# A four-layer attention kernel: the weighted sums of the one-head layer as seven products in three of four batches, joins taken ahead on the vector engine

## The chip, the core and the metric

The kernel is one program on one core of a Trainium2 chip. The core has a matrix engine (PE, with its weight loads shown as PEld), a vector engine (DVE), an activation engine (ACT), a general engine (POOL) and a queue for transfers (SP). [...] The metric is the device time of one execution in microseconds (us), as the median of some runs. A separate profiled execution gives the times of the single instructions. All data are float32.

## What is computed

The input x is [4, 512, 32, 32]: four batches of 512 channels by 1024 places. Four layers follow one another: attention with 8 heads, a linear attention, attention with one head after a layer normalisation, and attention with 4 heads after a group normalisation. The change lies in the third layer:

```python
def _L2_conv_ref(x, norm_w, w_qkv, b_qkv, w_proj, b_proj):
    b, c, h, w = x.shape
    xf = jnp.transpose(x, (0, 2, 3, 1)).reshape(b, h * w, c)
    mu = jnp.mean(xf, axis=-1, keepdims=True)
    var = jnp.var(xf, axis=-1, keepdims=True)
    xn = (xf - mu) * jax.lax.rsqrt(var + EPS) * norm_w
    qkv = jnp.einsum('bnc,dc->bnd', xn, w_qkv) + b_qkv
    q, k, v = jnp.split(qkv, 3, axis=-1)
    scale = c ** (-0.5)
    attn = jax.nn.softmax(jnp.einsum('bqc,bkc->bqk', q, k) * scale, axis=-1)
    out = jnp.einsum('bqk,bkc->bqc', attn, v)
    out = jnp.einsum('bnc,dc->bnd', out, w_proj) + b_proj
    out = jnp.transpose(out.reshape(b, h, w, c), (0, 3, 1, 2))
    return x + out
```

For one batch the weighted sum `attn @ v` is a product of a 1024 x 1024 matrix and a 1024 x 512 matrix.

## The kernel before

`plain_path` runs the layers one after the other, and within a layer batch after batch. The third layer is the loop over batches at L1555; its attention is `one_head` (L1128). There the projections are folded together beforehand: `gq` is the product of the query and key weights, `hv` that of the value and output weights. So a batch of this layer has four stages on PE:

1. `seven_products` with `gq`: the transformed queries `q` (PE line L701).
2. `project_v` (which calls `seven_products`): the values `vt`, already through the output weights (L819).
3. `seven_products` in `one_head`: the scores, keys by queries (L826). As soon as a block of scores is whole, `exp` puts its exponential in its place (ACT, L1146) and adds it to a running sum `acc` (DVE, L1149), from which the row sums come.
4. the weighted sums (L1168): a loop over 2 halves of the queries (`qb`) and 4 blocks of 128 output channels (`m`); each of its eight rounds is a chain of 8 matrix products of 128 x 128 by 128 x 512, one for each tile of 128 keys. After the first round two more products with `ones` spread the row sums over the partitions (L1175). DVE then inverts them (`invert`: a reciprocal L673 and two maxima L675 and L676 for a check), multiplies each round's result by the inverse (L1181) and adds bias and residual into x (L1183).

`seven_products` is a scheme in which a product of matrices of 2 x 2 blocks takes seven block products and not eight: `sum_inputs` and `sum_weights` make sums and differences of blocks (t[0..3] and s[0..3]), `p1` to `p7` are the block products, and DVE joins their results (L730 in `join`, L766 in `p6`, L771 in `p7`). It is used in stages 1 to 3; stage 4 is a direct product.

PE is scheduled by hand: `tc.manual_schedule(engines={PE})` keeps the order in which the program calls matrix products. For the other engines a scheduler picks, out of what is ready by its own clock, by a priority that follows the program's order. Small pieces of other work are put between PE's products in two ways: a list `pieces`, of which `slot()` takes one, and in `one_head` a list `parts`, of which one is taken ahead of each of the eight rounds. In stage 4 the parts are the layer normalisation of the next batch (`layer_norm`: `add`, `center`, `scale`, for each half), then `sum_inputs` for it; in the last batch the first group normalisation of the next layer, the load of that layer's weights `wqkv3` and the sum `weighted_bias("bo3", ...)`.

On chip memory is full, so tiles are shared by tags: the scores lie in the four "pt" tiles, the two "sum" tiles and the "wo" tile; `places`, the sums of the query blocks, lie before the change in the tile `after` that the next batch's normalisation writes. PSUM has four accumulator tiles of 512 columns (`acc_tile`) and two of twice that size (`two_tile`). Between batches `away(b)` stores x of a batch to a home in memory and `back` loads another one in its place (SP queue).

The two lines of stage 4 that matter most:

```python
out, lhsT=v[j // 2][:, j % 2, bass.ts(m, P)], rhs=pts[j][:, qb, :],
start=(i == 0), stop=(i == NT - 1),
```

Of the kernel before, what the change touches and what calls it, by code (L numbers as in the profile page):

```python
# [18 lines left out]
P = 128  # L19
# [455 lines left out]
def plain_path(ctx: ExitStack, tc: tile.TileContext, d: dict, out: bass.AP, count):  # L475
# [23 lines left out]
    def acc_tile():  # L499
        return ps_acc.tile([P, TB], F32, tag="acc", name="acc")  # L500
# [21 lines left out]
    def chunks_tile(tag, name, bufs=1):  # L522
        return work.tile([P, NC, TB], F32, tag=tag, bufs=bufs, name=name)
# [134 lines left out]

    idle = lambda: None

    def both(*fs):
        return lambda: [f() for f in fs]

# [41 lines left out]
    def seven_products(  # L705
# [20 lines left out]

        def join(out, ps, i, o, other):

            if bias is None:
                nc.vector.tensor_tensor(out, view(ps), other, ALU.add)  # L730
            else:
                joined[:] = [stt(out, view(ps), bias(i, o), other, ALU.add, ALU.add).ins]

        def p1(o, ms=(0, 1)):
            if 0 in ms:
# [27 lines left out]
        def p6(o):  # L763
            ps = acc_tile()
            mult(o, ps, made[o][1], t[1])
            nc.vector.tensor_tensor(dst(0, 1, o), dst(0, 1, o), view(ps), ALU.add)  # L766

        def p7(o):
            seven[o] = acc_tile()
            mult(o, seven[o], made[o][2], t[2], stop=False)  # L770
            nc.vector.tensor_tensor(dst(1, 1, o), dst(0, 1, o), view(seven[o]), ALU.add)  # L771


        if first:
# [350 lines left out]
        while parts:  # L1125
            parts.pop(0)()

    def one_head(b, q, ws, acc, keys, sums, v, scale, bias, parts):  # L1128

        x = xs[b]
        wide = wpool.tile([P, NC, C], F32, tag="wo", name="pts")
        pts = [pt_tile("pt") for _ in range(4)] + [sum_tile("pt") for _ in range(2)]
        pts += [wide[:, 2 * i : 2 * i + 2, :] for i in range(2)]

        order = [j for o in range(NC) for j in (o, o + NC)]  # L1140
        pts = dict(zip(order, pts))
        taken = []

        def exp(tb, o):
            pt = pts[tb * NC + o]
            nc.scalar.activation(pt, pt, AF.Exp, scale=scale)  # L1146
            taken.append(pt)
            if len(taken) > 1:
                nc.vector.tensor_tensor(acc, acc if len(taken) > 2 else taken[0], pt, ALU.add)  # L1149

        seven_products(
            NC,
            lambda i, j, o: q[i][:, 2 * j : 2 * j + 2, :],
            keys,
            None,
            lambda i, tb, o: pts[tb * NC + o][:, i, :],
            lambda: sums,
            lambda o: ws,
            keys_first,
            done=exp,  # L1160
        )
        quotients = chunks_tile("q0", "rd")
        for n, (qb, m) in enumerate(itertools.product(range(NTB), range(NC))):
            if parts:
                parts.pop(0)()
            out = acc_tile()
            for i, j in enumerate(order):
                nc.tensor.matmul(  # L1168
                    out, lhsT=v[j // 2][:, j % 2, bass.ts(m, P)], rhs=pts[j][:, qb, :],
                    start=(i == 0), stop=(i == NT - 1),  # L1170
                )
            if n == 0:
                ps = two_tile("rowsum")
                for t in range(NTB):
                    nc.tensor.matmul(  # L1175
                        ps[:, t, :], lhsT=ones, rhs=acc[:, t, :], start=True, stop=True
                    )
            if m == 0:
                invert(quotients[:, qb, :], ps[:, qb, :])
            t = quotients[:, NTB + n % 2, :]  # L1180
            nc.vector.tensor_tensor(t, out, quotients[:, qb, :], ALU.mult)  # L1181
            xv = x[:, m, bass.ts(qb, TB)]
            nc.vector.scalar_tensor_tensor(xv, t, bias[:, m : m + 1], xv, ALU.add, ALU.add)  # L1183
        assert not parts

# [168 lines left out]
    def layer_norm(b, tb, tiles):  # L1356

        x = xs[b][:, :, bass.ts(tb, TB)]
        t = {}

        def add():
            s = t["s"] = row_tile("s")
            nc.vector.tensor_tensor(s, x[:, 0, :], x[:, 1, :], ALU.add)
            for c in range(2, NC):
                nc.vector.tensor_tensor(s, s, x[:, c, :], ALU.add)

        def center():
            xn = tiles[tb]
            t["ps"] = two_tile("lnsums")
            mean = t["ps"][:, 0, :]  # L1370
            nc.tensor.matmul(mean, lhsT=ones, rhs=t["s"], start=True, stop=True)
            for c in range(NC):
                nc.vector.scalar_tensor_tensor(
                    xn[:, c, :], mean, -1.0 / C, x[:, c, :], ALU.mult, ALU.add
                )
            for c in range(NC):
                sq = row_tile("sq")
                nc.scalar.activation(sq, xn[:, c, :], AF.Square)
                if c == 0:
                    t["sq"] = sq  # L1380
                else:
                    nc.vector.tensor_tensor(t["sq"], t["sq"], sq, ALU.add)

        def scale():
            xn = tiles[tb]
            var = t["ps"][:, 1, :]
            nc.tensor.matmul(var, lhsT=ones, rhs=t["sq"], start=True, stop=True)
            rstd = row_tile("rstd")
            nc.scalar.activation(rstd, var, AF.Sqrt, bias=eps, scale=1.0 / C)
            nc.vector.reciprocal(rstd, rstd)  # L1390
            for c in range(NC):
                nc.vector.scalar_tensor_tensor(
                    xn[:, c, :], xn[:, c, :], col("nw2", c), rstd, ALU.mult, ALU.mult
                )

        return [add, center, scale]


    affine = {}
# [61 lines left out]
    with tc.manual_schedule(engines={mybir.EngineType.PE}):  # L1461
# [66 lines left out]
        lin = linear_attention(B - 1, lambda i: pt_tile("l1"))  # L1528

        norms[1][0]()  # L1530
        pieces.extend([norms[0][2], norms[1][1], *lin[:2], norms[1][2], idle, *lin[2:]])
        gq = chunks_tile("ot", "gq")
        for o in range(NC):
            ps = gps.get(o)
# [20 lines left out]
        for b in range(B):  # L1555
            q = q_tiles()
            vt = v_tiles()
            after = normed_tiles(b + 1)

            def sums():  # L1560
                if b == 0:
                    made.extend(sum_inputs(spare, normed(xn)))
                return made

            half = NC // 2
            seven_products(
                half,
                lambda i, j, o: gq[:, 2 * j : 2 * j + 2, bass.ts(i * half + o, P)],
                normed(xn),
                lambda i, o: uq[:, i * half + o : i * half + o + 1],  # L1570
                lambda i, tb, o: q[tb][:, i * half + o, :],
                sums,
                slots=2,
            )


            pair = lambda t, i: t[:, 2 * i : 2 * i + 2, :]
            places = [pair(after[0], 0), pair(after[0], 1), pair(after[1], 0), pair(q[1], 0)]
            query_sums = lambda: sum_weights(places, lambda i, j: pair(q[i], j))
            if b > 0:  # L1580
                query_sums()
            project_v(vt, hv, normed(xn), made, wpool.tile([P, NC, C], F32, tag="wo", name="ws"))
            flush()
            if b == 0:

                query_sums()
                away(B - 1)
                back(2)
            if b + 1 < B:
                norms = [layer_norm(b + 1, tb, after) for tb in range(NTB)]  # L1590
                (add0, *n0), (add1, *n1) = norms
                add0()
                parts = [
                    n0[0], idle, both(n0[1], add1), idle, n1[0], idle, n1[1],
                    lambda: sum_inputs(spare, normed(after)),
                ]
            else:
                first = chunks_tile("ot", "gn")

                def load3():  # L1600
                    return load_wqkv(d["wqkv3"]), load_bias(
                        d["bv3"], d["wo3n"],
                        [after[1][:, 2 * i : 2 * i + 2, :] for i in range(2)],
                    )

                loads3 = []
                norm = group_norm(0, 0, first)
                parts = [
                    idle, both(lambda: loads3.extend(load3()), norm[0]), *norm[1:],
                    lambda: loads3.append(weighted_bias("bo3", loads3.pop())),  # L1610
                ]
            one_head(
                b, q, places, pair(after[1], 1), normed(xn), made, vt, float(C) ** -0.5, bo2, parts
            )
            away(b)
            back((b + 3) % B)
            if b + 1 < B:
                xn = after
# [103 lines left out]
```

## Time and profile before

| what | us |
|---|---|
| median of 3 runs | 2511.36 |
| lowest and highest of them | 2510.95, 2512.14 |
| the profiled execution, its own time | 2511.6 |
| span in its profile, first to last instruction | 2509.5 |
| DVE busy in the span | 1606.4 |
| ACT busy | 705.3 |
| POOL busy | 255.2 |

The profiled execution took 2511.6 us, 2.1 us more than the span from its first to its last instruction, and 0.24 us more than the median of the runs. A matrix product in float32 is two entries of the profile, each of them with its own weight load. "Busy" of PE counts the time in which at least one product is under way; the entries overlap at their ends, so that the start-to-start distance, and not the length of an entry, is the price of one more product. The granted clock of PE is full (1.000) over the whole span.

### The profile page before, as it was taken

The numbers are of one execution on the slowest core, as the hardware profiler recorded it, in microseconds if no ns is written. First come the engines' busy times: TensorE is split into PE (matmuls) and PEld (weight loads), VectorE is DVE, ScalarE is ACT, GpSimd is POOL, SyncE is SP. The second block draws the span as 40 slices with busy tenths as digits, with TensorE's granted clock in tenths as the row PEclk, the third lists the DMA queues.
The fourth block names the chain that finished last, engine by engine and source line by source line (L and its number), as shares of the span: only waits on it lengthen the run. The fifth ranks groups of instructions, "written<-read, shape, count | busy, mean of one in ns | idle before, by whom it ended". The sixth has DMA issues, their size and how long they took to land.

```text
span 2509.5 us, 24916 instructions
## 1 busy us (share of the span) xinstructions
PE 2489.5 (99%) x10266; PEld 1286.6 (51%) x10266; DVE 1606.4 (64%) x1815; ACT 705.3 (28%) x859; POOL 255.2 (10%) x240
## 2 busy tenths in 40 slices
PE   9999999999999999999999999999999999999998
PEld 4545544554455454644645446446556456555653
DVE  3788588758875888657275463644664773565465
ACT  1454155315531643221120211102321320321121
POOL 4001100110020001102103011021010001002000
PEclk9999999999999999999999999999999999999999
DMA  5000010001000301011001010110000000000000
GB/s 214 1 1 1 5 68 1 1 5 68 1 1 17 115 1 51 5 67 56 12 1 67 0 70 2 67 67 17 17 31 20 1 17 17 1 17 17 0 9 26
DMA packets 23304, 72.46 MB, mean 29 GB/s; under 512 B 1809, under 2 KB 9489, under 8 KB 21137
## 3 DMA queue, kind: packets, MB, share of 16 engines
q1 hardware_dynamic: 23184, 70.82, 7.7%
q8 instruction: 82, 1.34, 0.2%
q14 instruction: 38, 0.30, 0.0%
HBM read 44.60 MB, written 25.17 MB: 28 GB/s over the span
## 4 chain that ended last, share of the span: by engine, by line
PE 96%; DVE 3%; issue 1%; ACT 0%; DMA 0%; SPq 0%; DVEq 0%; ACTq 0%
PE acc L701 19%; PE acc L819 12%; PE acc L1168 9%; PE acc L951 9%; PE sc L913 9%; PE sc L908 8%; PE acc L936 8%; PE acc L826 7%; PE acc L1013 6%; PE acc L963 1%; PE acc L971 1%; PE feat L638 1%; DVE sum L924 1%; PE acc L638 1%; DVE rd L673 1%; PE acc L1260 1%
## 5 line engine op out<-in xcount | busy, mean ns | idle before, releaser
L917 ACT ACTIVATE pt<-sc 128x1024 f32<-128x1024 f32 x384 | 380.3, 1023 | 631.7 <-PE sc L913 372.7
L924 DVE TENSOR_TENSOR sum<-sum,pt 128x1024 f32<-128x1024 f32 x256 | 313.2, 1224 | 46.7 <-ACT pt L917 35.3
L936 PE MATMUL acc<-pt,v 64*64 64x512 f32 x2048 | 291.1, 590 | 0.0
L908 PE MATMUL sc<-q,k 64*64 64x512 f32 x2048 | 273.9, 591 | 1.1 <-ACT pt L917 1.1
L913 PE MATMUL sc<-q,k 128*128 128x512 f32 x512 | 240.0, 593 | 0.7 <-ACT pt L917 0.7
L951 PE MATMUL acc<-pt,v 128*128 128x512 f32 x512 | 239.9, 592 | 0.0
L689 POOL TENSOR_TENSOR ws<-wqkv 128x256 f32<-128x256 f32 (+1 forms) x40 | 40.8, 1021 | 1343.2 <-PE acc L963 552.3
L673 DVE RECIPROCAL rd<-acc 128x512 f32<-128x512 f32 x32 | 107.4, 3357 | 107.4 <-PE acc L971 107.4
L701 PE MATMUL acc<-t,ws 128*128 128x512 f32 x384 | 173.9, 593 | 0.0
L1168 PE MATMUL acc<-pt,v 128*128 128x512 f32 x384 | 170.2, 592 | 0.0
L936 PEld LDWEIGHTS acc<-pt,v 64*64 64x64 f32 x2048 | 104.2, 133 | 121.3 <-issue 98.3
L908 PEld LDWEIGHTS sc<-q,k 64*64 64x64 f32 x2048 | 101.1, 133 | 123.6 <-issue 92.4
L951 PEld LDWEIGHTS acc<-pt,v 128*128 128x128 f32 x512 | 97.3, 190 | 122.5 <-issue 120.5
L913 PEld LDWEIGHTS sc<-q,k 128*128 128x128 f32 x512 | 96.7, 190 | 113.8 <-issue 87.9
L1168 PEld LDWEIGHTS acc<-pt,v 128*128 128x128 f32 x384 | 72.8, 190 | 90.9 <-issue 89.2
L701 PEld LDWEIGHTS acc<-t,ws 128*128 128x128 f32 x384 | 72.5, 190 | 86.6 <-issue 84.9
L673 DVE RECIPROCAL rd<-rs 128x512 f32<-128x512 f32 x32 | 107.3, 3353 | 1.1
L921 DVE TENSOR_TENSOR sum<-pt 128x1024 f32<-128x1024 f32 x64 | 76.7, 1198 | 42.7 <-ACT pt L917 42.7
L739 ACT COPY v<-acc 128x512 f32<-128x512 f32 x24 | 14.1, 586 | 287.9 <-PE acc L819 287.9
L730 DVE TENSOR_TENSOR v<-acc,v 128x512 f32<-128x512 f32 x72 | 49.7, 691 | 65.9 <-PE acc L819 65.7
L819 PE MATMUL acc<-ws,t 128*128 128x256 f32 x384 | 87.3, 379 | 0.0
L826 PE MATMUL acc<-q,ln 128*128 128x512 f32 x192 | 85.9, 593 | 0.8 <-DVE pts L730 0.8
(272 smaller groups left out, 3513.0 us busy)
## 6 DMA issues: line engine op xcount, KB each, us to landing
home<-x SPq DMA_DIRECT2D x8, 2048.0 KB, 6.3
x<-home SPq DMA_DIRECT2D x8, 2048.0 KB, 7.9
out<-x SPq DMA_DIRECT2D x32, 256.0 KB, 2.1
x<-in_x SPq DMA_DIRECT2D x3, 2048.0 KB, 16.9
wo<-in_wo SPq DMA_DIRECT2D x3, 1024.0 KB, 5.4
w<-in_w SPq DMA_DIRECT2D x1, 3072.0 KB, 17.6
wqkv<-in_wqkv SPq DMA_DIRECT2D x1, 3072.0 KB, 11.3
wqkv<-in_wqkv SPq DMA_DIRECT2D x2, 1024.0 KB, 9.6
```

Of the source, the lines that this page charges most:

```text
L673: nc.vector.reciprocal(rd, ps)
L701: nc.tensor.matmul(ps, lhsT=w[:, m, :], rhs=x[:, m, :], start=start, stop=stop, skip_group_check=True)
L819: nc.tensor.matmul(ps[:, bass.ts(r, C // 2)], lhsT=x[:, m, bass.ts(2 * o + r, P)], rhs=w[:, m, :], start=(start and r == 0), stop=stop, sk ...
L826: nc.tensor.matmul(ps, lhsT=x[:, m, bass.ts(o, P)], rhs=w[:, m, :], start=start, stop=stop, skip_group_check=True,)
L908: nc.tensor.matmul(ps[half(h), s, :], lhsT=key(g, i)[half(s), half(h)], rhs=q[qb][half(s), g, :], start=True, stop=True,)
L913: nc.tensor.matmul(ps[:, s, :], lhsT=key(g, 2 * i + s), rhs=q[qb][:, g, :], start=True, stop=True)
L917: exps.append(nc.scalar.activation(pt, ps, AF.Exp, scale=scale).ins)
L924: nc.vector.tensor_tensor(acc, acc, pt, ALU.add)
L936: nc.tensor.matmul(outs[qb, g][r][half(s), :], lhsT=v[i // 2][half(r), i % 2, g * P + s * hd : g * P + (s + 1) * hd], rhs=pt[half(r), s, : ...
L951: nc.tensor.matmul(outs[qb, g][0], lhsT=v[j // 2][:, j % 2, bass.ts(g, P)], rhs=pt[:, s, :], start=(j == 0), stop=(j == NT - 1),)
L1013: nc.tensor.matmul(ps[i][:, bass.ts(o, n)], lhsT=w[:, m, bass.ts(o, P)], rhs=t[:, m, :], start=(start and m + o == 0), stop=(stop and m == ...
L1168: nc.tensor.matmul(out, lhsT=v[j // 2][:, j % 2, bass.ts(m, P)], rhs=pts[j][:, qb, :], start=(i == 0), stop=(i == NT - 1),)
```

## The change

- In batches 1, 2 and 3 of the third layer, stage 4 becomes a scheme of seven block products: the blocks are two halves of the keys, two halves of the queries and two halves of the output channels. Each block product is a chain of 4 matrix products of 128 x 128 by 128 x 512 for each of two blocks of 128 output channels. Batch 0 keeps the direct product with its `parts`.
- The sums and differences of the blocks are made on DVE (`each`): 16 instructions of 128 x 256 for the values, 16 of 128 x 512 for the exponentials. They are put into tiles that are free by then (`xn`, `room`, the query tiles) or in place.
- The row sums come after `p1` and `p2` (after 16 products, where it was after 8); the four blocks' results are joined in SBUF (`add`), multiplied and added to x by `add_block`.
- In batches 1 and 2 the next batch's layer normalisation moves from stage 4 to `pieces`, taken from stage 2 on; `sum_inputs` for the next batch comes after stage 4. In batch 3 the group normalisation, the load of the bias weights and `weighted_bias` move there too; the load of `wqkv3` stays at the start of stage 4.
- The query sums `places` and the running sum `acc` get tiles of their own. `layer_norm` splits `scale` into `spread` and `scale`.
- The joins in all of `seven_products` (L730, L766, L771 before) and the `add`s are issued under `soon()`, which raises their priority for the scheduler.

The core of the diff:

```diff
+    soon = lambda: tc.high_priority(offset=300)
...
-            if bias is None:
-                nc.vector.tensor_tensor(out, view(ps), other, ALU.add)
-            else:
-                joined[:] = [stt(out, view(ps), bias(i, o), other, ALU.add, ALU.add).ins]
+            with soon():
+                if bias is None:
+                    nc.vector.tensor_tensor(out, view(ps), other, ALU.add)
+                else:
+                    joined[:] = [stt(out, view(ps), bias(i, o), other, ALU.add, ALU.add).ins]
...
+        n = C // 2
+        quotients = [xn[1][:, t, :] for t in range(NTB)]
+        temps = [xn[0][:, t, :] for t in range(4)]
+        d, e = temps[:2], temps[2:]
+        quarter = lambda t: t.rearrange("p a (r m) -> p (a r) m", m=n)
+        ws = [quarter(t) for t in (xn[1][:, 2:4, :], room[1][:, :2, :], room[1][:, 2:4, :])]
+        ts = [chunks_tile("q0", "ts"), room[0], None, chunks_tile("q1", "ts")]
+        weights = lambda i, j: [v[2 * j + m // 2][:, m % 2, i * n : (i + 1) * n] for m in range(4)]
+        inputs = lambda j, tb: [pts[4 * j + m][:, tb, :] for m in range(4)]
...
+        def each(out, a, b, op):
+            for args in zip(out, a, b):
+                nc.vector.tensor_tensor(*args, op)
...
+            for m in range(4):
+                nc.tensor.matmul(
+                    ps[i, o], lhsT=w[m][:, bass.ts(o, P)], rhs=t[m],
+                    start=(start and m == 0), stop=(stop and m == 3), skip_group_check=True,
+                )
...
+        def p3(o):
+            mult(5, o, s4, inputs(1, 1), start=False)
+            add(d[o], d[o], ps[5, o])
+            finish(0, 1, o, d[o], d[o])
+        def p4(o):
+            mult(7, o, weights(1, 1), t4, start=False)
+            add(e[o], d[o], ps[7, o])
+            finish(1, 0, o, e[o], e[o])
+        def p5(o):
+            mult(5, o, s1, t1, stop=False)
+            add(e[o], e[o], ps[5, o])
+            finish(1, 1, o, e[o], e[o])
+        def p6(o):
+            mult(6, o, s2, t2)
+            add(d[o], d[o], ps[6, o])
+        def p7(o):
+            mult(7, o, s3, t3, stop=False)
+            add(e[o], d[o], ps[7, o])
+        p1(0)
+        p1(1)
+        each(s1, weights(1, 0), weights(1, 1), ALU.add)
+        each(s2, s1, weights(0, 0), ALU.subtract)
+        each(t1, inputs(0, 1), inputs(0, 0), ALU.subtract)
+        each(t2, inputs(1, 1), t1, ALU.subtract)
+        p2(0)
+        p2(1)
+        rows = row_sums()
+        for t in range(NTB):
+            invert(quotients[t], rows[:, t, :])
+        for o in range(2):
+            finish(0, 0, o, e[o], ps[1, o])
+        each(s3, weights(0, 0), weights(1, 0), ALU.subtract)
+        each(t3, inputs(1, 1), inputs(0, 1), ALU.subtract)
+        each(t4, inputs(1, 0), t2, ALU.subtract)
+        each(s4, weights(0, 1), s2, ALU.subtract)
+        for f, o in [
+            (p6, 0), (p7, 0), (p6, 1), (p5, 0), (p4, 0), (p7, 1), (p3, 0), (p5, 1), (p4, 1), (p3, 1)
+        ]:
+            f(o)
...
-        return [add, center, scale]
+        return [add, center, spread, scale]
...
+            halves = work.tile([P, 2, 2, TB], F32, tag="os", name="qs")
+            third = work.tile([P, 2, TB], F32, tag="oi", name="qs")
+            places = [halves[:, 0], halves[:, 1], third, pair(q[1], 0)]
+            sum_weights(places, lambda i, j: pair(q[i], j))
...
+            elif b + 1 < B:
+                pieces.extend([
+                    add0, n0[0], idle, n0[1], n0[2], add1, n1[0], idle, n1[1], n1[2],
+                ])
             else:
                 first = chunks_tile("ot", "gn")
...
+                pieces.extend([
+                    *group_norm(0, 0, first),
+                    lambda: loads3.append(weighted_bias("bo3", loaded3)),
+                ])
...
+            if 0 < b < B - 1:
+                sum_inputs(spare, normed(after))
             away(b)
             back((b + 3) % B)
```

## The prediction

> **What bounds the kernel now.** I read the busy shares first, then the chain that ended last, then PE's instructions in order of time in the stage that changes.
>
> ```profile
> PE 2489.5 (99%) x10266; PEld 1286.6 (51%) x10266; DVE 1606.4 (64%) x1815; ACT 705.3 (28%) x859; POOL 255.2 (10%) x240
> ...
> PEclk9999999999999999999999999999999999999999
> ...
> PE 96%; DVE 3%; issue 1%; ACT 0%; DMA 0%; SPq 0%; DVEq 0%; ACTq 0%
> ```
>
> PE is busy for all but 20 us of the span, at full clock, and the chain runs through PE for 96%. A share of 99% can hide gaps between pipelined entries, so I look at the starts, here from the end of the scores of batch 2 to the next batch's first products (start, length, what, how many entries):
>
> ```profile
> 1431.07 1.02 PE L1371 MATMUL lnsums<-s,ones 128*128 128x512 f32 x2
> 1431.92 5.31 PE L1168 MATMUL acc<-pt,v 128*128 128x512 f32 x12
> 1437.07 1.88 PE L1168 MATMUL acc<-pts,v 128*128 128x512 f32 x4
> 1438.79 1.88 PE L1175 MATMUL rowsum<-ln,ones 128*128 128x512 f32 x4
> ...
> 1491.15 7.03 PE L701 MATMUL acc<-ln,gq 128*128 128x512 f32 x16
> ```
>
> From 1431.92 to 1438.79 are 16 entries, so one entry costs 0.429 us and one product (two entries) 0.858 us. From 1431.07 to 1491.15, 60.08 us, there are 8 rounds of 16 entries, 4 of row sums and 8 of the normalisation: 140 x 0.429 = 60.06. There is no gap at all: the stage costs what its number of products costs. [...]
>
> DVE's load and its relation to PE, by stretch (scores, then weighted sums, of batch 2) and by price:
>
> ```profile
> 1382.90:1431.07 48.17, 48.17 (x115) 21.36 (x114) 19.07 (x25) 13.04 (x16) 0.00 (x0) 1.00 0.00 0
> 1431.07:1491.15 60.08, 60.08 (x142) 26.60 (x140) 48.20 (x54) 9.08 (x13) 2.33 (x2) 1.00 0.01 5
> ```
> ```profile
> L673 DVE RECIPROCAL rd<-rowsum 128x512 f32<-128x512 f32 x8 | 26.8, 3354 | 10.5 <-PE rowsum L1175 10.5
> ...
> L766 DVE TENSOR_TENSOR pt<-pt,acc 128x512 f32<-128x512 f32 x12 | 8.3, 688 | 63.2 <-PE acc L826 63.2
> ...
> L1309 DVE TENSOR_TENSOR kxt<-kxh 128x256 f32<-128x256 f32 x8 | 3.0, 420 | 2.2 <-ACT kxh L1305 2.2
> ```
>
> The third number is DVE: 19.07 of 48.17 us in the scores, 48.20 of 60.08 in the weighted sums. So DVE is loaded in just the stage that gets more of its work.
>
> **The change, part by part.**
>
> *Products removed.* The weighted sums of a batch are 8 x 8 = 64 products; seven block products are 7 x 2 x 4 = 56. Row sums and normalisation keep their number, the latter only moves. So 8 products in each of 3 batches go: 24 x 0.858 = 20.6 us. As this stage has no gap, they come off the span unless PE waits for something new.
>
> *The sums on DVE.* Each batch gets 16 instructions of 128 x 512 and 16 of 128 x 256, and 10 joins. Back to back the starts are closer than the lengths: three starts in a row in this stage are 1456.62, 1457.22 and 1457.83, 0.60 us apart at 0.69 us each; a pair of the 128 x 256 form takes 0.75 us, so 0.33 for one more. The question is whether all sums are done when the row sums are, because the reciprocals are behind them in DVE's order as built. From the start of the scores' last ten products to the end of the row sums PE needs 10 x 2 + 16 + 2 = 38 products, 32.6 us. DVE has in that time 10 joins (6.0), 5 additions of 128 x 1024 to `acc` (starts 1.14 apart: 5.7), 32 sums (16 x 0.60 + 16 x 0.33 = 14.9) and 2 additions of the next normalisation (1.2): 27.8 us. Spare are 4.8 us, of which I give half to waits for products (DVE waits about 1 us between joins now). So nothing is lost. The other end: were each 128 x 256 to cost as much as 128 x 512, 4.3 us more, 1.9 would pass to PE, 5.7 in three batches. [...]
>
> *The division.* There are four accumulators. p1 and p2 hold two until DVE has the inverse; p6 and p7 take the other two; the second p6 takes the first one's after its join; the next product, p5, needs a bank of p1 and p2. PE gets there 12 products after the row sums: 10.30 us. DVE starts 0.20 us after the row sums (now 1440.71, PE's next start being 1440.51) and does, in the built order, reciprocal 3.27, maximum 0.55, the join of p6 0.60, maximum 0.58, reciprocal 3.27, maxima 0.55 and 0.58, and the product that frees the bank, 0.69: 10.29 us. That is a tie. I take 0.1 us per batch, 0.3 in all; what DVE is late before adds in full.
>
> *First products.* p1 needs the exponentials of keys 0 to 3 within 4 products, where the old order alternated halves. In batch 2 the last exponential of the first half started at 1430.35 (1.06 long), 0.34 us after the scores; it is needed after three products, 2.57 us. Hidden; no cost. With the cover gone it would be 1.06.
>
> *Normalisation moved.* Its PE products stay 4 a batch. Its DVE work (by starts: two reciprocals at 3.27, 8 scalings at 0.67, 8 centrings and 12 additions at 0.60 to 0.62: 24 us a batch) goes to `project_v` and the scores; in the latter alone DVE has 29 us of 48 free. In batch 1 the second mean product stands behind all products of `project_v`, and its channel sum behind the last joins on DVE: the ninth product's join ends 0.8 us after that product, two additions 1.3 us, while PE is there 1.73 us after it. I take 0.6 us; the ends are 0 and one reciprocal ahead of it, 3.3.
>
> *Moved transfers, batch 3.* The bias weights (2 x 512 KB) are now issued between `away` and `back`, and the DVE instruction that needs them stands early among the joins of `q`. Now it stands among the scores:
>
> ```profile
> 1584.21 0.69 DVE L555 SCALAR_TENSOR_TENSOR ln<-ln,bv 128x512 f32<-128x512 f32 x1 [1.03 <-DMA ln<-in_wo3n]
> 1586.71 1.98 PE L826 MATMUL acc<-q,ln 128*128 128x512 f32 x4 [0.84 <-DVE pts L730]
> ```
>
> DVE waited 1.03 us for the transfer, the joins behind it were late, and PE lost 0.84 us. That loss goes. In its new place DVE reaches it 8.8 us after x is stored; `away` lands in 6.3 us and 1 MB more at its rate is 3.1, so DVE may wait 0.6 us or more; the join of p6 is behind it, whose bank PE wants 5 us later. So -0.8, and 0 to 1 for the new place, taken as 0. The group statistics of x that `back` loads stand 15.6 us behind the store; the load lands 14.2 us after (6.25 to its issue, 7.9 to landing): hidden by 1.4 us. `wqkv3` (11.3 us) has the whole stage.
>
> *Other moves.* ACT gets 2 copies of 0.59 a batch in a stretch where it is nearly idle; POOL's sums for `places` start one stage earlier than needed. *Priorities:* DVE's order in the first two layers is as before, instruction for instruction, so the joins' priority acts in the third layer alone, within the sums above.
>
> Sum against the profiled execution: -20.6 + 0.3 + 0.6 - 0.8 = -20.5, so a span of 2489.0. The profiled run, 2511.6, is within 0.3 us of the runs' median; 2511.36 - 20.5 = **2490.9 us**.
>
> **Rivals.** *A, DVE a little late in each batch:* the division's tie passes every lateness on. For it: zero slack there. Against: spare time before. Price: the 5.7 of the dear small sums, 3.3 of the batch-1 wait instead of 0.6, and 1 of the transfer: 9.4 more, up to 2500.
>
> *B, DVE becomes the bound of the stage, and the kernel gets slower:* the sums of two SBUF operands would cost what POOL's rows show for such forms (1.27 for 128 x 512, 0.72 for 128 x 256, its sums after 1491 us). Then 16 x 0.67 + 16 x 0.39 = 17 us more before the division, less 2.4 spare: 14.6 a batch, 44 in three, about 2534. It decides from 8.5 us a batch ((20.5 + 5) / 3). Against it are DVE's own rows above, of the same forms.
>
> *C, the gain is given back:* waits for transfers stop DVE's joins. If both x loads took the 16.9 us of the first loads and the bias weights 11.3 instead of 3.8, DVE would be 7.6, 9 and 8 us late, PE, with two to three products in hand (some 4 us), 3.6 + 5 + 4 = 13: 2504. For it is the 0.84 above; against, that the queue is nearly empty in this layer. To end within 0.2% it would have to be yet a little worse.
>
> **How the numbers follow.** The forecast has 0.80, A 0.12, B 0.04, C 0.04. A measurement of this kernel tells about 0.2%, 5 us, from no change. Forecast and A are faster; C lies at the edge, counted half as same. Faster 0.93, same 0.03, slower 0.04. The range: below, no new wait and the runs' spread of 0.4 (2511.36 - 21.4 - 0.9 = 2489); above, most of A: 2501.
>
> **What would show it.** In the profile after: 7 x 16 + 4 = 116 entries, 49.8 us, from the first product of a changed stage to the next batch's first; the wait ahead of the first p5 at most 0.5 us; DVE idle for some 2 us ahead of the first reciprocal; DVE busy for some 80% of the stage, and yet PE without a gap; no wait of L826 in batch 3. I am wrong if p5 waits for over 2 us in each batch (A), if products are more than 0.43 us apart all through the stage (B), or if DVE waits on transfers by more than 3 us (C).

## The result, and the profile after

The changed kernel takes 2488.32 us (median of 4 runs, 2487.56 to 2488.9); the kernel before took 2511.15 us on the same chip. The ratio is 0.9908, with an interval of 0.9891 to 0.9925: 22.8 us less. The forecast of 2490.9 us lies 2.6 us above it. The direction and the main term are right, but the range began at 2489, and the time is 0.7 us below that. More was gained than the sum had terms for.

The page after, busy shares, clock and chain, as they were shown of before:

```profile
PE 2468.6 (99%) x10218; PEld 1277.3 (51%) x10218; DVE 1679.0 (68%) x1941; ACT 705.0 (28%) x863; POOL 253.6 (10%) x240
...
PEclk9999999999999999999999999999999999999999
...
PE 96%; DVE 3%; issue 1%; ACT 0%; DMA 0%; SPq 0%; DVEq 0%
```

PE has 48 entries fewer (24 products), DVE 126 instructions and 72.6 us more, and PE is still what bounds the kernel. The share of PE did not move: both span and work became shorter.

Two stretches of batch 1 after, scores and then weighted sums (length, then busy time and count of PE, PEld, DVE, ACT, POOL, then PE's clock):

```profile
1228.40:1277.30 48.90, 48.90 (x115) 21.66 (x114) 34.23 (x50) 15.65 (x21) 0.00 (x0) 1.00 0.00 0
1277.32:1327.24 49.92, 49.92 (x117) 21.96 (x116) 42.72 (x58) 2.67 (x4) 5.11 (x5) 1.00 0.00 0
```

The changed stage takes 49.92 us for 116 entries. At 0.429 us each these are 49.8, so all but some 0.15 us is products. DVE is busy for 86% of it, where some 80% was forecast, and PE has no gap that shows. The critical place of the stage is the division. PE's instructions there, then DVE's, in order of time:

```profile
1291.05 1.88 PE L1172 MATMUL rowsum<-acc,ones 128*128 128x512 f32 x4
1292.77 3.60 PE L1232 MATMUL acc<-w 128*128 128x512 f32 x8
...
1299.63 3.60 PE L1232 MATMUL acc<-w 128*128 128x512 f32 x8
1303.11 3.70 PE L1232 MATMUL acc<-ts,ln 128*128 128x512 f32 x8
```
```profile
1292.97 3.36 DVE L675 RECIPROCAL ln<-rowsum 128x512 f32<-128x512 f32 x1 [2.05 <-PE rowsum L1172]
...
1297.97 3.35 DVE L675 RECIPROCAL ln<-rowsum 128x512 f32<-128x512 f32 x1
...
1302.37 0.68 DVE L1179 TENSOR_TENSOR ln<-acc,ln 128x512 f32<-128x512 f32 x1
```

DVE stood idle for 2.05 us before the row sums came (some 2 us forecast). The product that frees the bank for p5 ends at 1303.05. Eight entries from 1299.63 put p5 at 1299.63 + 8 x 0.4293 = 1303.07, and it starts at 1303.11, its eight entries 0.1 us longer than those of a group without a wait. So the tie is there, and costs 0.14 us a batch.

The waits of PE that stand in one of the two lists alone, of before and then of after (who waited for whom: us in total, times, longest):

```profile
PE upd L1326 <- DVE x L1332: 0.9, 2, 0.7
PE acc L826 <- DVE pts L730: 0.8, 1, 0.8
...
PE sc L913 <- ACT pt L917: 0.7, 1, 0.7
```
```profile
PE lnsums L1481 <- DVE s L1475: 0.7, 1, 0.7
```

Three waits went, and one came. The prediction had the L826 wait and the new one (the second mean product of batch 1). It did not have the other two: the matrix products of the linear attention (`upd`), and the first exponential of the fourth layer.

The starts of the same PE instructions in both traces give the whole ledger:

| stretch | us gained |
|---|---|
| the first load of weights, up to PE's first entry | 0.36 |
| PE's first eight entries | 0.30 |
| from the ninth entry up to 1060 us, in small steps | 0.13 |
| the two updates of the linear attention | 1.01 |
| batch 1: 8 products (6.87), less the new wait and the tie | 5.75 |
| batch 2: 8 products, less the tie | 6.73 |
| batch 3: 8 products, and the L826 wait, less the tie | 7.89 |
| first scores of the fourth layer | 0.94 |
| behind the end of PE's last entry | 0.60 |
| difference of the spans (2509.5 - 2485.8) | 23.7 |

Three of these lines (0.36, 0.30 and 0.60) are no larger than what changes from run to run. Over the traces of all the kernels here, which begin and end alike, PE's first entry starts at 4.20 to 5.79 us, its first eight entries take 4.98 to 6.56 us, and from the end of its last entry to the end of the span pass 5.89 to 6.63 us. Without the two ends, from the start of PE's ninth entry to the start of its last one, PE needed 2491.93 us before and 2469.48 after, 22.45 us less. In the control below, the same kernel run again, this stretch is 2469.47 us. It tells kernels apart more finely than the medians, whose runs often spread over 1 to 2 us, and is called PE's stretch below.

### The profile page after: what moved, and what is told of

Read it like the earlier page. It is cut to its first block, busy times and chain, and to the rows that moved or that the text cites. A ratio compares the mean times of both kernels' runs of the same rounds, so it can differ in the third digit from the quotient of the medians.

```text
span 2485.8 us, 24942 instructions
## 1 busy us (share of the span) xinstructions
PE 2468.6 (99%) x10218; PEld 1277.3 (51%) x10218; DVE 1679.0 (68%) x1941; ACT 705.0 (28%) x863; POOL 253.6 (10%) x240
## 4 chain that ended last, share of the span: by engine, by line
PE 96%; DVE 3%; issue 1%; ACT 0%; DMA 0%; SPq 0%; DVEq 0%
PE acc L703 20%; PE acc L824 11%; PE sc L918 9%; PE acc L956 9%; PE sc L913 8%; PE acc L941 8%; PE acc L831 8%; PE acc L1018 6%; PE acc L1232 6%; PE acc L1193 2%; PE acc L968 1%; PE acc L976 1%; PE feat L638 1%; DVE sum L929 1%; PE acc L638 1%; DVE rd L675 1%
## 5 line engine op out<-in xcount | busy, mean ns | idle before, releaser
L913 PE MATMUL sc<-q,k 64*64 64x512 f32 x2048 | 273.7, 591 | 1.1 <-ACT pt L922 1.1
L956 PE MATMUL acc<-pt,v 128*128 128x512 f32 x512 | 239.9, 592 | 0.0
L913 PEld LDWEIGHTS sc<-q,k 64*64 64x64 f32 x2048 | 101.1, 133 | 123.6 <-issue 92.4
L956 PEld LDWEIGHTS acc<-pt,v 128*128 128x128 f32 x512 | 97.3, 190 | 122.5 <-issue 120.5
L831 PE MATMUL acc<-qs,w 128*128 128x512 f32 x192 | 86.6, 593 | 0.0
L742 ACT COPY q<-acc 128x512 f32<-128x512 f32 x40 | 23.4, 585 | 207.8 <-PE acc L703 207.8
```

Of the source, the lines that this page charges most:

```text
L831: nc.tensor.matmul(ps, lhsT=x[:, m, bass.ts(o, P)], rhs=w[:, m, :], start=start, stop=stop, skip_group_check=True,)
L913: nc.tensor.matmul(ps[half(h), s, :], lhsT=key(g, i)[half(s), half(h)], rhs=q[qb][half(s), g, :], start=True, stop=True,)
L956: nc.tensor.matmul(outs[qb, g][0], lhsT=v[j // 2][:, j % 2, bass.ts(g, P)], rhs=pt[:, s, :], start=(j == 0), stop=(j == NT - 1),)
```

## The experiments

Differences are against the unchanged after-kernel of the first set, 2488.41 us. Between the three sets the kernel before moved from 2511.63 to 2511.21 and 2511.11, so differences of medians across sets are good to some 0.5 us.

**The products alone.** The control is the changed kernel as it is.

> The changed kernel again, untouched, as the common base of the runs beside it. Expected: 2488.3 us (2487.5 to 2489.0), and PE's first product 4.3 to 4.7 us after the first instruction; how far that start and the total move from run to run is the share of the missed 2.3 us that no theory of the kernel needs to explain.

It took 2488.41 us (2487.29 to 2489.0), ratio 0.9908, interval 0.9893 to 0.9923. The time is as expected; PE's first product started 4.77 us after the first instruction, just outside the 4.3 to 4.7 expected. Beside it a kernel that keeps everything of the change, but computes the weighted sums directly in all batches:

```diff
-            parts = []
+            parts = [idle]
```

> Batches 1 to 3 take the direct product again, everything else stays as changed. Theory R (24 products are worth 20.6 us as predicted, and the missed 2 us come from the rest of the change): 2488.3 + 20.6 - 0.4 (the wait ahead of p5 goes) = 2508.5, some 2.5 us under the kernel before. Rival P (a product removed is worth more than 0.858 us, 22.8 / 24 = 0.95): 2511, the time of before.

It took 2508.85 us (2507.73 to 2509.5): 20.4 us over the control, ratio to before 0.9989 (0.9980 to 0.9998). PE's stretch is 20.15 us longer than the control's. That is theory R, and not P. The seven products with their sums, joins and division are worth 20.4 us, against 20.6 - 0.3 in the prediction. All the rest of the change is worth 2511.63 - 2508.85 = 2.8 us, where the prediction's terms gave 0.2 (0.8 less 0.6).

**The two waits that the prediction had not costed.** In the diff `flush()`, which empties the list `pieces`, moves from behind `project_v` to a place behind the scores in `one_head`. So the second `update` of the linear attention, still in the list when `project_v` of batch 0 ends, stood right behind the first one and now comes at a slot among the scores. Putting it back (the store and the load of x that end the list come earlier with it):

```diff
             project_v(vt, hv, normed(xn), made, wpool.tile([P, NC, C], F32, tag="wo", name="ws"))
+            if b == 0:
+                flush()
             one_head(
```

> In batch 0 the pieces are flushed directly after the values again, as before the change. Theory U (the two updates of x of the linear attention stood next to each other before and the second waited for DVE to free its PSUM tile; now a stretch of scores lies between them): PE waits at the update again, 0.7 + 0.2 us and two restarts of 0.1: 1.0 us slower than the control, 2489.3. Rival J (the missed part is jitter of the start): as the control.

It took 2489.55 us (2488.65 to 2490.16), 1.14 us over the control. The runs of the two overlap, so the trace has to decide: PE's stretch is 0.95 us longer. Its waits and its PE instructions at the place:

```profile
PE upd L1436 <- DVE x L1442: 0.9, 2, 0.7
```
```profile
1064.23 1.99 PE L1436 MATMUL upd<-block 64*128 64x512 f32 x8
1066.90 1.13 PE L1436 MATMUL upd<-block 64*128 64x512 f32 x4 [0.68 <-DVE x L1442]
1068.22 1.13 PE L1436 MATMUL upd<-block 64*128 64x512 f32 x4 [0.19 <-DVE x L1442]
```

The second group of updates needs the banks that DVE is still emptying. In the changed kernel it starts 19 us later, without a wait:

```profile
1064.35 1.99 PE L1436 MATMUL upd<-block 64*128 64x512 f32 x8
...
1083.63 1.99 PE L1436 MATMUL upd<-block 64*128 64x512 f32 x8
```

The other one is on ACT. The group norm of the fourth layer's first batch takes a square root on ACT. Before, it came in stage 4 behind the last exponentials of batch 3; now it comes ahead of them. A square root of one column behind that stage restores the old sequence of functions:

```diff
+            if b == B - 1:
+                dummy = small.tile([P, 1], F32, tag="dummy", bufs=1, name="dummy")
+                nc.scalar.activation(dummy, xs[b][:, 0, 0:1], AF.Sqrt, bias=eps, scale=0.0)
             away(b)
```

> One square root of 128 x 1 on ACT behind the third layer's last batch, which nothing reads. Theory T (the group normalisation's square root now comes ahead of the last exponentials, so the next layer's first exponential finds its table loaded; before it had to load it, 1.28 us, and PE waited 0.73 us): a table load of 1.28 us ahead of the first exponential of the fourth layer, PE waits 0.7 to 0.9 us there, 0.9 us slower than the control: 2489.2. Rival J: as the control.

It took 2489.56 us (2488.51 to 2490.15), 1.15 us over the control, and PE's stretch is 0.99 us longer. ACT in this kernel, the first row, against the changed kernel, the second, and PE's wait in this kernel:

```profile
1698.07 1.28 ACT L922 ACT_TABLE_LOAD   x1 [18.43 <-PE sc L918]
```
```profile
1697.72 1.02 ACT L922 ACTIVATE pt<-sc 128x1024 f32<-128x1024 f32 x1 [18.45 <-PE sc L918]
```
```profile
1700.44 1.13 PE L918 MATMUL sc<-q,k 128*128 128x512 f32 x2 [0.72 <-ACT pt L922]
```

Here a table load of 1.28 us stands between the square root and the next exponential. PE waited 0.72 us for that exponential, and its next two entries took 1.13 us, where two without a wait take 1.02. ACT had been idle for 18 us when it happened; the idle time did not help, since this load came only when the scores were there. A load need not come so late: that of the extra square root, in the same trace, ran at once behind the instruction before it, and the square root then waited 18.45 us for its input.

```profile
1581.63 1.28 ACT L1732 ACT_TABLE_LOAD   x1
1601.36 0.29 ACT L1732 ACTIVATE dummy<-x,eps 128x1 f32<-128x1 f32 x1 [18.45 <-DVE x L1181]
```

Why the one waits and the other does not, no run here shows.

**How much room DVE has, and where.** One extra reciprocal of 3.35 us, once behind both divisions and once ahead of the row sums (its result is overwritten):

```diff
         for t in range(NTB):
             invert(quotients[t], rows[:, t, :])
+        nc.vector.reciprocal(e[0], rows[:, 0, :])
```

> One more reciprocal of 128 x 512 (3.27 us by its starts) on DVE between the division and the product that frees the bank for p5, in each of the three batches; nothing reads it. Theory D (the division and PE's twelve products are a tie, so lateness passes in full): 3 x 3.27 = 9.8 us slower than the control, 2498.1, PE waiting 3.2 to 3.4 us ahead of p5 in each batch. Rival H (other work of PE or another bank hides it): under 3 us in all.

```diff
         each(t2, inputs(1, 1), t1, ALU.subtract)
+        nc.vector.reciprocal(e[0], inputs(1, 1)[3])
         p2(0)
```

> The same extra reciprocal, but ahead of the row sums, among the sums of the exponentials. Theory D (DVE has spare time there: it sat idle for 2.05 us ahead of the first reciprocal in batch 1 and 3.38 in batch 2): 1.2 us slower in batch 1 and nothing or little in the others, 2489.5. Rival F (DVE is full all through the stage, so the place of an instruction does not matter): 9.8 us slower, as the run with the reciprocal behind the row sums.

The early one took 2488.79 us (2488.52 to 2489.04), 0.4 us over the control: 3 x 3.35 us of DVE work nearly for nothing. The late one took 2504.65 us (2499.06 to 2505.89), 16.2 us over it. So the place decides, and the tie passes on all that comes behind the row sums. But 16.2 is more than the 9.8 expected, although PE's wait, 3.08 us, is close to the 3.2 to 3.4 expected (late kernel, waits; then its PE rows):

```profile
PE acc L1232 <- DVE ln L1242: 9.3, 3, 3.1
```
```profile
1300.72 3.60 PE L1232 MATMUL acc<-w 128*128 128x512 f32 x8
1307.40 5.40 PE L1232 MATMUL acc<-ts,ln 128*128 128x512 f32 x8 [3.08 <-DVE ln L1242]
1312.63 3.60 PE L1232 MATMUL acc<-ts,v 128*128 128x512 f32 x8
```

Behind the gap of 3.08 us the same eight entries take 5.40 us, and not 3.60. The granted clock tells why (late kernel, two stretches; columns as above, with the DMA share and GB/s at the end):

```profile
1300.00:1307.40 7.40, 4.32 (x11) 1.57 (x10) 7.40 (x6) 0.00 (x0) 0.00 (x0) 1.00 0.00 0
1307.40:1312.80 5.40, 5.40 (x9) 2.41 (x10) 5.40 (x8) 0.00 (x0) 0.00 (x0) 0.68 0.01 3
```

The clock was 0.68 of full speed over those 5.40 us: 0.32 x 5.40 = 1.7 us lost. In batches 2 and 3 of that run the eight entries took 6.64 and 5.34 us. With the three waits, 9.3, and what the three groups take over the 3.60 of one without a wait, 6.6, this gives 15.9; the spans differ by 2502.7 - 2487.1 = 15.6.

**The priority of the joins.**

```diff
-    soon = lambda: tc.high_priority(offset=300)
+    soon = lambda: nullcontext()
```

> The joins lose their priority, the scheduler places them by the program's order again; everything else as changed. Theory Q (joins behind sums on DVE hold back accumulators and the division): DVE's order as built has joins behind 128 x 512 sums, so that PE waits 0.5 to 0.8 us several times in the values and scores and some 3 us ahead of p5 in each batch: 10 to 13 us slower, 2498 to 2501. Rival N (with spare time on DVE the order does not matter): within 1 us of the control.

It took 2503.09 us (2502.5 to 2505.82), 14.7 us over the control, a little above what was expected. Its waits:

```profile
PE acc L1232 <- DVE ln L1179: 8.1, 3, 2.7
...
PE acc L824 <- DVE v L733: 2.1, 2, 1.6
...
PE acc L831 <- DVE pt L733: 1.1, 2, 0.6
...
PE acc L831 <- DVE pts L733: 0.6, 2, 0.3
```

Without priority DVE does both divisions through to the end before the join of the first p6, so PE stands for 2.71 us in each batch already at the second p6. The rest is joins in stages 2 and 3 that wait behind the moved normalisation and, at the end of the scores, behind the sums. Some seven tenths of the products' gain (14.7 of 20.4 us) hang on the order in which DVE takes its work. In batch 2 alone the clock was lowered again: 5.21 us for the eight entries behind the 2.71 us, where batches 1 and 3 show 3.70.

**The lost clock.** The late kernel with half an extra reciprocal, and with two of them:

```diff
+        nc.vector.reciprocal(e[0][:, :256], rows[:, 0, :256])
```

> The extra reciprocal behind the second division, at half its width (128x256 instead of 128x512). Width halves its duration to an estimated 1.7 us (half of the 3.35 us row), so by the wait of 3.08 us that the full one left, the wait in each of three batches should be 3.08 - 1.65 = 1.4 us. Theory G (TensorE's clock drops only behind a gap of some 3 us; behind gaps of 2.71 us it dropped in one of three, so the edge lies about there): the eight entries behind each wait take 3.70 us as behind any short wait, and the time is the unchanged kernel's 2488.4 + 3 x (1.4 + 0.1) = 2492.9 us (2492.0 to 2494.0). Rival H (the loss comes with any such wait, whatever its length): 5.4 us for those eight entries and 2498.3 us.

```diff
+        nc.vector.reciprocal(e[0], rows[:, 0, :])
+        nc.vector.reciprocal(e[0], rows[:, 1, :])
```

> The extra reciprocal at full width, twice (3.35 us each), behind the second division. The wait in each of three batches should be 3.08 + 3.27 = 6.35 us. Without any lowered clock the time would be 2488.4 + 3 x 6.45 = 2507.8 us. Theory G, one fixed loss of some 1.8 us behind each gap that is long enough: 2513.2 us (2511.5 to 2516.0). Rival J, the loss grows with the length of the gap (twice the gap, some 3.6 us): 2518.6 us.

The half took 2493.0 us (2492.87 to 2493.74), as expected to the tenth: three waits of 4.5 us in total, the first of 1.48 us with 3.70 us for its eight entries at a granted clock of 1.00, and 1.000 over the whole run. The double took 2510.16 us (2508.32 to 2511.98): above the 2507.8 without a lowered clock, and below the range of theory G. Its premise failed (PE's rows in batch 1):

```profile
1307.13 5.11 PE L1232 MATMUL acc<-ts,ln 128*128 128x512 f32 x8 [3.08 <-DVE ln L1242]
1314.59 3.70 PE L1232 MATMUL acc<-ts,v 128*128 128x512 f32 x8 [2.35 <-DVE ln L1242]
```

The scheduler put the second reciprocal behind the first output, so there are two gaps instead of one long one in batches 1 and 2 (in batch 3 the slow entries cover the second). What a longer gap costs stays open. But it gives two more lengths: behind 3.08 us the clock fell again in all three batches (0.72, 0.71 and 0.54 over the eight entries), behind 2.35 and 2.28 us it did not (3.70 us for the eight entries, and behind 2.35 a clock of 1.00).

The length of the gap alone does not decide, though; theory G is wrong in that: behind the three equal gaps of 2.71 us in the kernel without priority, the eight entries took 5.21 us once and 3.70 twice. In the late kernel the drops of the clock, at 1307.46, 1461.06 and 1614.66 us, are 153.60 us apart, 45 times 3.413, and each lasts 3.41 or 6.83 us. Cut into windows of 3.413 us, of which one is the drop of its clock, the kernel without priority shows what differs between its equal gaps (batch 2, three windows; then batch 1, two; the first time behind the comma is PE's, the clock the third number from the end):

```profile
1456.10:1459.51 3.41, 1.03 (x3) 0.19 (x1) 3.41 (x4) 0.00 (x0) 0.00 (x0) 1.00 0.00 0
1459.51:1462.92 3.41, 3.08 (x4) 1.51 (x5) 2.79 (x5) 0.00 (x0) 0.00 (x0) 0.50 0.02 5
1462.92:1466.33 3.41, 3.41 (x9) 1.48 (x8) 2.96 (x4) 0.00 (x0) 0.00 (x0) 1.00 0.00 0
1299.08:1302.49 3.41, 2.31 (x6) 0.76 (x4) 3.41 (x2) 0.00 (x0) 0.00 (x0) 1.00 0.00 0
1302.49:1305.90 3.41, 1.80 (x4) 0.87 (x5) 3.41 (x7) 0.00 (x0) 0.00 (x0) 1.00 0.00 0
```

In batch 2 most of the gap fell into one window, PE worked for 1.03 us of it, and the next window ran at 0.50 of the clock. In batch 1 the same gap was split between two windows, with 2.31 and 1.80 us of work, and the clock stayed at 1.00. So it is in the traces of the late kernel, the one without priority and the double: seven windows with 0.33 to 1.20 us of work were followed by a halved clock, and no window with 1.80 us or more was, as long as the clock was full. A gap of 1.48 us leaves at least 3.41 - 1.48 = 1.93 us of any window for work, so the kernel with half a reciprocal fits this as well as it fits theory G.

**Taking out the two small losses.**

```diff
-        for t in range(NTB):
-            invert(quotients[t], rows[:, t, :])
+        invert(quotients[0], rows[:, 0, :])
         for o in range(2):
             finish(0, 0, o, e[o], ps[1, o])
+        invert(quotients[1], rows[:, 1, :])
...
-                    add0, n0[0], idle, n0[1], n0[2], add1, n1[0], idle, n1[1], n1[2],
+                    add0, n0[0], idle, n0[1], add1, n0[2], n1[0], idle, n1[1], n1[2],
```

> The changed kernel with two reorderings alone: finish(0, 0) of both outputs between the two divisions, and the additions for the second mean one piece earlier. The waits at the fifth product (0.04 + 0.1 us of restart in each of three batches, 0.4 us) and at the second mean's product (0.71 + 0.2 us in batch 1) should go: 2488.4 - 0.4 - 0.9 = 2487.1 us (2486.5 to 2487.8). Rival: the waits only move to the next instruction behind, 2488.4 us.

It took 2487.01 us (2486.73 to 2488.08), ratio 0.9905 (0.9890 to 0.9920). The waits at L1481 and at p5 are gone from its trace:

```profile
1227.40 1.02 PE L1481 MATMUL lnsums<-s,ones 128*128 128x512 f32 x2
```
```profile
1302.93 3.60 PE L1232 MATMUL acc<-ts,ln 128*128 128x512 f32 x8
```

The gain of 1.4 us over the control is as expected, but it is across sets; PE's stretch, which leaves out the two ends, is 1.27 us shorter.

**Seven products in batch 0 too.** With both reorderings, the sums of weights of batch 0 on POOL, and the normalisation of batch 1 spread over slots of the new scheme:

```diff
             if b == 0:
-
-                parts = [
...
+                pieces.extend([add0, n0[0], idle, idle, n0[1], n0[2], add1]); late.extend([idle]*6 + [n1[0], idle, idle, n1[1], n1[2]])
...
-        each(s1, weights(1, 0), weights(1, 1), ALU.add)
...
+        each(s1, weights(1, 0), weights(1, 1), ALU.add, pool=b == 0)
...
-            if 0 < b < B - 1:
+            if b < B - 1:
                 sum_inputs(spare, normed(after))
```

> Seven products in batch 0 too, with the value sums of that batch on POOL, the second half of the next normalisation spread behind the products, one half's division ahead of the other's, and the channel sums of the second half ahead of the scaling of the first. If the price of a product holds and no new wait comes: -6.9 us for eight products, -0.4 for the wait ahead of p5, -1.0 for the wait of the second mean in batch 1: 2480.1. Rival (POOL's sums are too slow beside DVE, or DVE becomes the bound in batch 0, where the normalisation, the sums and the division lie in 98 us): PE waits in batch 0 alone, up to 6 us, 2484 to 2487.

It took 2482.95 us (2482.04 to 2483.6), 5.5 us under the control and not 8.3. One miss shows as a new wait at the next batch's queries: DVE, without a pause from 1130 to 1187 us, is late with the sums.

```profile
PE acc L703 <- DVE q L776: 1.3, 1, 1.3
```

Among that DVE work are the three additions for batch 2's first mean (2.0 us), which are not needed for a long time. On POOL:

```diff
+            e = nc.gpsimd if (b, tb) == (2, 0) else nc.vector
             s = t["s"] = row_tile("s")
-            nc.vector.tensor_tensor(s, x[:, 0, :], x[:, 1, :], ALU.add)
+            e.tensor_tensor(s, x[:, 0, :], x[:, 1, :], ALU.add)
             for c in range(2, NC):
-                nc.vector.tensor_tensor(s, s, x[:, c, :], ALU.add)
+                e.tensor_tensor(s, s, x[:, c, :], ALU.add)
```

> The kernel of e8_batch0 with the three additions for batch 2's first mean (128x512, 0.68 us each on the vector engine) on GpSimd. Reading of e8's trace: the vector engine is never idle from 1130 to 1187 us, these additions stand 2.0 us long in that run at 1160.39, and TensorE waits 1.29 us at 1186.96 for the subtraction at the end of it. If that is so, the wait goes, and the time is 2482.95 - 1.3 - 0.1 = 2481.5 us (2481.0 to 2482.3). Rival: the additions on GpSimd slow the vector engine's own instructions beside them by as much as they save, 2482.9 us.

It took 2481.75 us (2481.15 to 2482.3), ratio to before 0.9882 (0.9867 to 0.9897), and the wait is gone. This is the fastest version here: 29.4 us under the kernel before, 6.7 under the changed one. By PE's stretch it is 7.14 us under the control, 1.2 short of the 8.3. Most of that stands in batch 0, where three groups of PE start late:

```profile
1117.16 1.98 PE L831 MATMUL acc<-q,w 128*128 128x512 f32 x4 [0.19 <-DVE pts L776]
...
1143.26 3.70 PE L1233 MATMUL acc<-w 128*128 128x512 f32 x8
...
1158.03 1.13 PE L1511 MATMUL lnsums<-sq,ones 128*128 128x512 f32 x2
```

By the starts ahead of them they are 0.35, 0.25 and 0.07 us late, and each is 0.1 us longer than a group without a wait: 1.0 us.

## Why the prediction was right, and where it was not

*Products removed* (-20.6) was right. The rule that an entry without a gap costs its start-to-start distance held: the direct kernel differs by 20.4 (20.15 in PE's stretch), tie and all.

*The sums on DVE* (0) was right. DVE was idle for 2.05 us before the row sums in batch 1, and the reciprocal put ahead of them cost 0.4 us in three batches. The prices by starts (0.60 and 0.33) held: in the trace after, sums of 128 x 512 start at 1272.99 and 1273.59 us, 0.60 apart, and a pair of 128 x 256 again takes 0.75 us. That speaks against the ends of rivals A and B, which priced them dearer.

*The division* (+0.3) was right as a mechanism, a tie, and measured 0.14 a batch, 0.42 in all. 0.04 of it is the wait; 0.1 is a restart that had no term of its own.

*First products* (0): no wait shows ahead of p1.

*Normalisation moved* (+0.6): the wait of 0.71 us came at the place named. With what a wait costs beyond its row it makes 0.98 us; together with the tie the batch lost 1.12.

*Moved transfers* (-0.8): the L826 wait went, and batch 3 gained 1.16 us beside its products. In the new place DVE waited 0.78 us for the bias weights, where 0 to 1 was allowed, and no wait of PE took the place of the old one.

So these three terms were off by 0.1 to 0.4 us each, and the misses nearly cancel (+0.1 forecast, +0.24 measured); that is luck. They have mostly one source: a wait shown as 0.7 us costs PE some 0.27 us more, because the row counts idle time from the modelled end of the last entry, 0.59 us after its start, where the next would have started after 0.43, and because the group behind it is 0.1 us longer.

*Other moves* is the step that failed. It listed ACT's two copies and POOL's sums and set them at nothing. It left out two moves that the diff shows: `flush()` behind `project_v`, with an `update` of the layer before in its list, and group norm's square root past batch 3's exponentials. Both had a row in the trace of before: the `upd` waits of 0.9 us and the 0.7 us wait of the first L913. They bring 1.0 and 0.9 us by PE's starts in the two traces, and putting one back costs 0.95 and 0.99 us of PE's stretch (1.14 and 1.15 by the medians). With 1.9 us for them the sum goes from -20.5 to -22.4, and PE's stretch became 22.45 us shorter; with the 2.3 of the medians it goes to -22.8, which is the difference of the medians.

The *range* failed by that and by its own rule. Its lower end leaves out the two new waits (0.9 us) and takes another 0.9 us off for a spread that it gives as 0.4. It gave nothing for gains not found, though a move can remove a wait by accident as well as add one. The chances do not quite follow their own rule either: with half of C as same, they would be 0.94 for faster and 0.02 for same.

Of the rivals, A's chain (the tie passes lateness on) is true, as the late reciprocal shows, but DVE is not late. Its price would have been too low once a wait reaches some 2.7 us: a lowered clock came on top of one wait of 2.71 us in three (5.21 us for the eight entries, not 3.70) and of all six of 3.08 us. B did not occur: DVE at 86% in the stage does not bound it. C did not occur, and no run made the transfers slower.

## What to carry to other kernels

When PE has no gap, price a removed product by the distance of starts, and then go through every wait of PE in the trace of before and ask of each whether the diff moves either side of it. Moves that look like book-keeping (a list that is emptied later, a square root ahead of an exponential) were worth some 2 of 22.8 us here. In a stage where another engine is 86% busy, what counts is what stands behind the last dependency: 3.35 us of DVE work cost 0.1 us a batch ahead of the row sums and over 5 behind them, and the priority of the joins was worth 14.7 us. For differences of 1 us compare the starts of the same instructions in two traces, without the first microseconds and the last.

## What the hardware showed that was not expected

PE's clock was lost behind gaps for which no expectation of the first runs had a term, and the loss came near the wait itself: up to 3.0 us behind 3.08. In the profiled executions above, behind gaps of 1.48, 1.49, 2.28 and 2.35 us the eight entries took 3.70 us; the granted clock was 1.00 behind the 1.48 and the 2.35. Behind 2.71 us they did so twice and took 5.21 us once, at a granted clock of 0.70. Behind 3.08 us they took 5.11 to 6.74 us in six cases of six, at 0.54 to 0.72, so 1.4 to 3.0 us more. Cut into windows of 3.413 us as above, PE had worked for 0.33 to 1.20 us in the window ahead of each drop, and from a full clock none came behind a window with 1.80 us or more. In these traces the edge lies somewhere between 1.20 and 1.80; where, they do not show.

The price fits the lengths of the drops. The clock stayed at half for 3.41 or 6.83 us, and PE lost half of the time that it worked in them: in batch 1 of the late kernel all of 3.41 us, so 1.7 us (5.40 us for the eight entries, not 3.70). The equal gaps of 2.71 us differed in where they fell in their windows; that this place differs from run to run is my estimate, which no trace shows. It would fit that the late kernel's runs spread from 2499.06 to 2505.89 us, at granted clocks of 0.998 to 0.996, where the control's stay within 1.7. The lowest of them is 10.65 us over the control, little more than its three waits alone cost, and its granted clock, 0.998, is the highest of them; so six cases of six are not a rule for gaps of 3.08 us.
